# Seven half products for layer 0 too, and sums made in PSUM on a bank already copied out

## The chip, the cores and the metric

One core of a Trainium2 chip runs the whole kernel. The metric is the device time of the program in microseconds (us); lower is better. TensorE multiplies matrices and writes to PSUM[...]; VectorE and ScalarE read PSUM; GpSimd computes a power for the normalizations; SyncE issues the DMAs.

## The reference

There are 32 graphs of 512 nodes with 128 features, and one weighted adjacency matrix `adj` (512 x 512), the same for all graphs. Four layers follow one another, each as `x = x + layer(relu(layernorm(x)))`, all in fp32:

```python
# layer 0: graph convolution
A_hat = adj + eye;  d = A_hat.sum(-1) ** -0.5
out = einsum('nm,bmc->bnc', d[:, None] * A_hat * d[None, :], x) @ W.T + b
# layer 1: gated recurrence, five steps
m = einsum('nm,bmd->bnd', adj, h);  av = concat([m, m])
u3 = h @ u3_w.T + u3_b
z = sigmoid(av @ w3_w.T + w3_b + u3);  r = sigmoid(av @ w4_w.T + w4_b + u3)
hv = tanh(av @ w5_w.T + w5_b + (r * h @ u5_w.T + u5_b));  h = (1 - z) * h + z * hv
# layers 2 and 3: masked attention (softmax over the edges), layer 2 with elu
```

So each graph is multiplied by a 512 x 512 matrix once in layer 0 (normalized adjacency, `anT` in the kernel) and five times in layer 1 (`adj` itself, `adjT`).

## The kernel before, in words

**Plan.** The program is not written in the order in which it runs. Each step is given to `op(engine, cost, due, emit, r, w)`: the engine, an assumed cost in us, a due number, the instruction, what it reads and what it writes. `Plan.run` (lines 81 to 148) then plays the program through once, with these costs and with fixed delays between engines (line 47): whenever an engine is free it takes, of its operations whose inputs are ready and for which a buffer is free, the one with the lowest due number, and among equal ones the one that was given first. That fixes the order of each engine's queue; on the chip each engine runs its queue in that order and waits where an input is late. Buffers are drawn from named lists (lines 170 to 200), among them eight PSUM banks, seven `h`, seven `m`, six `half`, two `S`, three `y`, four `z`, nine `hT`.

**Order of the work.** Lines 712 to 718 give the graphs in 16 pairs `b, b+1`: layer 0 (`gcn`) for each of the two, layer 1 (`ggnn`) for the pair, then the two attention layers (`gat`) for each. Due numbers rise by 10 from pair to pair and by 6 (`LANES`) from one step of layer 1 to the next, and six lanes (one for each graph that is in layer 1) let three pairs be in layer 1 at once. Layer 0 of pair b has due numbers from 5b - 10 on; the first pair's is far earlier. The last four graphs' attention takes a way without DMAs (`near`). 

**Layer 0.** `gcn` (line 470) normalizes x into y (`norm_relu`, one ScalarE instruction for each of four chunks of 128 nodes), adds the bias to x, and calls `product` (line 460): four matmuls of 128 x 128 by 128 x 512 (line 464), one for each chunk of y, are added up in one PSUM bank, and ScalarE copies the bank to m (line 466). Four small matmuls with `w0T` (line 480) and one VectorE add (line 482) finish.

**Layer 1.** `products` (line 503) multiplies the states h of both graphs of a pair at once. Each h is cut into two halves of 256 nodes, and `adjT` into four quarters. Instead of the eight half products that this takes, seven are made, of sums and differences: VectorE makes four sums `S` of halves of the two h (line 515); the right factors are three quarters of `adjT` as they are (`PLAIN`, line 301) and four differences of quarters, made once (`half_adj`, lines 299 to 312). A half product is two matmuls of 128 x 128 by 128 x 256 (line 528) into the low half of a bank. The results are put together as follows; k is the number of the half product:

- bank r1: product 0, copied to `p1` by ScalarE (538); then product 3 is added on top in PSUM, and ScalarE copies the sum to the low half of m1 (544);
- bank r2: product 1; VectorE makes `u2 = p1 + r2` (540). Then product 4 afresh; VectorE makes the high half of m2 as `u4 + r2` (546). Then product 6 on top; the low half of m2 is `u2 + r2` (550);
- bank r3: product 2; `u4 = u2 + r3` (542). Then product 5 on top; the high half of m1 is `u2 + r3` (548).

So a layer-1 product has nine VectorE instructions (four S, five sums) and two ScalarE copies. VectorE's have a due number 5 below that of the matmuls.

`step` (line 553) then makes the gates: matmuls with m and h^T (lines 557 to 572), tanh on ScalarE (560, 566, 574), products on VectorE (562, 576 to 579). The new state goes through VectorE transposes and two rounds of DMA (`shuttle`, line 435) to become the next h.

**Start.** adjT, the degree sums, anT (lines 291 and 294) and the factors of adjT (310, due -6) are made in the first 21 us, while x is still being loaded; the masks of the attention layers follow (323 to 332, due 6 and 7).

Of the kernel before, what the change touches and what calls it, by code (L numbers as in the profile page):

```python
# [14 lines left out]
P = 128  # L15
EPS = 1e-5
STEPS = 5
# [5 lines left out]
LANES = 6  # L23
# [128 lines left out]
def gnn_stack(ctx: ExitStack, tc: tile.TileContext, a: dict, out: bass.AP):  # L152
    nc = tc.nc
    x, adj = a["x"], a["adj"]
    B, N, D = x.shape
    C = N // P
# [6 lines left out]
    def tiles(n, shape, name, pool=sb, dtype=F32):  # L163
        return [pool.tile(shape, dtype, name=f"{name}_{next(serial)}") for _ in range(n)]

    def flat(t):
        return t.rearrange("p c k -> p (c k)")

    TOKENS, SMALL = [P, C, D], [P, C]
# [1 line left out]
        "bank": tiles(8, TOKENS, "bank", psum),  # L171
        "lane": list(range(LANES)),
        "x": tiles(13, TOKENS, "x"),
        "h": tiles(LANES + 1, [P, 2, 2 * D], "h"),
        "sq": tiles(2, [P, Q, W * C], "sq"),
        "far": tiles(4, [Q, W, Q, W * C], "far", dram),
        "hT": tiles(LANES + 3, TOKENS, "hT"),
        "y": tiles(3, TOKENS, "y"),
        "m": tiles(LANES + 1, TOKENS, "m"),
        "S": tiles(2, [P, 4, 2 * D], "S"),  # L180
        "half": tiles(6, [P, 2 * P], "half"),
        "r": tiles(2, TOKENS, "r"),
        "rh": tiles(4, TOKENS, "rh"),
        "z": tiles(4, TOKENS, "z"),
        "hv": tiles(2, TOKENS, "hv"),
        "gT": tiles(2, [P, Q, W * C], "gT"),
        "h_gat": tiles(3, [P, C, D + 3], "h_gat"),
# [13 lines left out]
    op = plan.op  # L201
    MM, MM1, TURN = 0.858, 0.224, 0.111
    V, A = 0.61, 0.585

    def fixed(shape, name, parts=1, dtype=F32):
        v = Val(None, parts)
        v.t = tiles(1, shape, name, dtype=dtype)[0]
        return v
# [81 lines left out]
    for m in range(C):  # L290
# [4 lines left out]
            block(anT.t, m), ident.t, dinv2.t[:, m:m + 1], block(anT.t, m), op0=ALU.mult, op1=ALU.add),  # L295
           r=[ident, dinv2], w=[anT[m]])


    half_adj = fixed([P, 4, 2, 2 * P], "half_adj", 4)
    FACTOR = (None, 1, 0, None, 2, None, 3)  # L300
    PLAIN = {0: (0, 0), 3: (1, 0), 5: (1, 1)}

    def quarter(a, n):
        return adjT.t[:, 2 * a:2 * a + 2, n * 2 * P:(n + 1) * 2 * P]

    def right(k):
        return quarter(*PLAIN[k]) if k in PLAIN else half_adj.t[:, FACTOR[k]]

    for k, u, v in ((2, (0, 1), 0), (1, (1, 1), 2), (4, (1, 1), None), (6, (1, 0), 1)):
        op("DVE", 0.62, -6, lambda k=k, u=u, v=v: nc.vector.tensor_sub(  # L310
            right(k), quarter(*u), quarter(0, 1) if v is None else right(v)),
           r=[adjT, *([half_adj[FACTOR[v]]] if v else [])], w=[half_adj[FACTOR[k]]])


    maskT = {l: fixed([P, Q, N], f"maskT{l}", C, dtype=BF16) for l in (2, 3)}
# [102 lines left out]

    def chunk(h, c):

        if h.kind != "h":
            return h.t[:, c, :]
        return h.t.rearrange("p a (f l) -> p a l f", l=2)[:, c // 2, c % 2, :]

# [10 lines left out]
    def shuttle(src, squares, dst, halves, due, soon):  # L435
# [19 lines left out]
        else:  # L455
            op("SP", 0.4, due, lambda: nc.sync.dma_start(
                dst.t if dst.kind != "h" else dst.t.rearrange("p a (k f) -> p (a k) f", k=2), far.t.rearrange("q i k f -> (q i) k f")),
               r=[far], w=[dst], delay=5)

    def product(h, mT, due):  # L460

        p, m = Val("bank"), Val("m")
        for c in range(C):
            op("PE", MM, due, lambda c=c: nc.tensor.matmul(flat(p.t), chunk(h, c), mT.t[:, c, :], start=(c == 0), stop=(c == C - 1)),  # L464
               r=[h[c] if len(h.writers) > 1 else h, mT[c]], w=[p, m])
        op("ACT", A, due, lambda: nc.scalar.copy(flat(m.t), flat(p.t)), r=[p], w=[m])
        return m


    def gcn(b, due):  # L470
        xb, y = xs[b], Val("y", C)
        norm_relu(b, y, due if b > 1 else 2 * b - 798)
        op("DVE", V, due + 1, lambda: nc.vector.tensor_add(xb.t, xb.t, b0.t[:, None, :].to_broadcast([P, C, D])),
           r=[b0], w=[xb])
        m = product(y, anT, due + 1)
        p = Val("bank")

        def out_mm():
            for c in range(C):
                nc.tensor.matmul(p.t[:, c, :], m.t[:, c, :], w0T.t[:, 0, :], start=True, stop=True)  # L480
        op("PE", C * MM1, due + 2, out_mm, r=[m, w0T], w=[p])
        op("DVE", V, due + 2, lambda: nc.vector.tensor_add(flat(xb.t), flat(xb.t), flat(p.t)), r=[p], w=[xb])


    def ggnn(pair, due):
        hs, hTs, lanes = [], [], []
        for b in pair:
            lane, h, hT = Val("lane"), Val("h", 2), Val("hT")
            op("SP", 0.0, due - 3, lambda: None, r=[xs[b]], w=[lane], delay=0)
            op("SP", 0.0, due - 3, lambda: None, r=[lane], w=[h], delay=0)  # L490
            norm_relu(b, h, due - 3)
            p = to_features(h, due - 2, hT)
            op("ACT", A, due - 2, lambda p=p, hT=hT: nc.scalar.copy(flat(hT.t), flat(p.t)), r=[p], w=[hT])
            hs.append(h)
            hTs.append(hT)
            lanes.append(lane)
        for s in range(STEPS):
            now = due + LANES * s
            ms = products(*hs, now)
            for i, b in enumerate(pair):  # L500
                hs[i], hTs[i] = step(b, s, ms[i], hTs[i], now + i, lanes[i])

    def products(h1, h2, due):

        x1, x2, S = (h1[0], h1[1]), (h2[0], h2[1]), Val("S", 4)
        HV, HM = 0.34, 2 * 0.43

        def part(item):  # L510
            v, a = item
            return v.t[:, a, :]

        def combine(o, u, v, f):
            op("DVE", HV, due - 5, lambda: f(part(o), part(u), part(v)), r=[u, v], w=[o])  # L515
        add, sub = nc.vector.tensor_add, nc.vector.tensor_sub
        combine(S[2], x1[0], x2[0], sub)
        combine(S[0], x2[0], x2[1], add)
        combine(S[1], S[0], x1[0], sub)
        combine(S[3], x1[1], S[1], sub)  # L520
        m1, m2, p1, u2, u4 = Val("m", 2), Val("m", 2), Val("half"), Val("half"), Val("half")
        r1, r2, r3 = Val("bank"), Val("bank"), Val("bank")

        def times(r, item, k, fresh, *also):
            def two():
                u = part(item).rearrange("p (f l) -> p l f", l=2)
                for l in range(2):
                    nc.tensor.matmul(flat(r.t)[:, :2 * P], u[:, l, :], right(k)[:, l, :], start=fresh and l == 0, stop=l == 1,  # L528
                                     skip_group_check=not fresh)
            op("PE", HM, due, two, r=[item, adjT if k in PLAIN else half_adj[FACTOR[k]]], w=[r, *also])  # L530

        def low(v):
            return flat(v.t)[:, :2 * P]

        def high(v):
            return flat(v.t)[:, 2 * P:]
        times(r1, x1[0], 0, True, m1, m2, p1, u2, u4)
        op("ACT", 0.35, due, lambda: nc.scalar.copy(p1.t, low(r1)), r=[r1], w=[p1])  # L538
        times(r2, S[1], 1, True)
        op("DVE", HV, due - 5, lambda: nc.vector.tensor_add(u2.t, p1.t, low(r2)), r=[p1, r2], w=[u2])  # L540
        times(r3, S[0], 2, True)
        op("DVE", HV, due - 5, lambda: nc.vector.tensor_add(u4.t, u2.t, low(r3)), r=[u2, r3], w=[u4])
        times(r1, x1[1], 3, False)
        op("ACT", 0.35, due, lambda: nc.scalar.copy(low(m1), low(r1)), r=[r1], w=[m1[0]])
        times(r2, S[2], 4, True)
        op("DVE", HV, due - 5, lambda: nc.vector.tensor_add(high(m2), u4.t, low(r2)), r=[u4, r2], w=[m2[1]])
        times(r3, S[3], 5, False)
        op("DVE", HV, due - 5, lambda: nc.vector.tensor_add(high(m1), u2.t, low(r3)), r=[u2, r3], w=[m1[1]])
        times(r2, x2[1], 6, False)
        op("DVE", HV, due - 5, lambda: nc.vector.tensor_add(low(m2), u2.t, low(r2)), r=[u2, r2], w=[m2[0]])  # L550
        return m1, m2

    def step(b, s, m, hT, due, lane):
        gate, r, rh, z = Val("bank"), Val("r"), Val("rh"), Val("z")
# [155 lines left out]


    for b in range(0, B, 2):
        gcn(b, STEPS * b - 10)
        gcn(b + 1, STEPS * b - 8)
        ggnn((b, b + 1), STEPS * b)
        for i in range(2):
            gat(b + i, 2, STEPS * (b + i) + LANES * (STEPS - 1) + 3)
            gat(b + i, 3, STEPS * (b + i) + LANES * (STEPS - 1) + 8)
# [32 lines left out]
```

The softmax here doesn't subtract the row's maximum and nothing guards it: scores larger than these inputs give would overflow.

## Time and profile before

| | |
|---|---|
| time, median of 3 runs (range) | 1669.84 us (1669.07 to 1671.38) |
| profiled execution: its own time | 1668.99 us |
| its span, first to last instruction | 1667.2 us |
| mean granted TensorE clock | 0.997 |
| plain products (L464) | 256 matmul records, 593 ns each |
| half products (L528) | 2240 matmul records, 379 to 381 ns each |
| chain that ended last | TensorE 96%, VectorE 3%, ScalarE 1% |

An fp32 matmul stands in the trace as two records; a matmul's duration is longer than its distance to the next one, because they are pipelined. In the lines, "L528 PE MATMUL bank<-half_adj,S" is line 528 of the kernel on TensorE (PE), writing a bank and reading half_adj and S; DVE is VectorE, ACT is ScalarE, PEld the load of the stationary matrix. "x4" means four records. In brackets stands how long the engine was idle before the instruction, and what it waited for. In the table by stretches each engine's busy time follows in its column, then the granted clock.

### The profile page before, as it was taken

What the parts mean: (1) busy time and instruction counts of PE and PEld (TensorE: products, weight loads), DVE (VectorE), ACT (ScalarE), POOL (GpSimd) and SP (SyncE); (2) the same over time, 40 slices, a digit from 0 to 9 for tenths busy, and PEclk for the clock granted to TensorE, in tenths of its full rate; (3) what the DMA queues carried; (4) which work ended last, traced back from release to release, by engine and by line L of the source; (5) the groups of instructions that cost most, each with busy time, mean ns of one, the idle gap of its engine ahead of it and who ended that gap; (6) DMA issues with size and microseconds to landing.
All of it is one profiled execution on the core that took longest, in us unless ns stands there. A gap on an engine that the chain in (4) does not pass through costs nothing.

```text
span 1667.2 us, 23457 instructions
## 1 busy us (share of the span) xinstructions
PE 1645.4 (99%) x7242; PEld 1141.2 (68%) x7242; DVE 1371.1 (82%) x3887; ACT 681.1 (41%) x1467; POOL 143.4 (9%) x136
## 2 busy tenths in 40 slices
PE   8999999999999999999999999999999999999998
PEld 5666656676766776767676676776767767775777
DVE  8866768789887887979889788897988879777988
ACT  5543443435344344443445434344443534334333
POOL 2200001001010010100101010010100001000100
PEclk9999999999999999999999999999999999999999
DMA  5132232353333434343342433424234433434110
GB/s 169 38 73 70 69 92 62 71 135 93 102 85 79 103 86 112 81 100 97 84 115 76 105 92 80 111 75 122 72 94 101 106 87 77 118 77 108 32 33 26
DMA packets 311422, 146.15 MB, mean 88 GB/s; under 512 B 150400, under 2 KB 292864, under 8 KB 311296
## 3 DMA queue, kind: packets, MB, share of 16 engines
q1 hardware_dynamic: 311008, 144.12, 34.3%
q8 instruction: 57, 0.93, 0.2%
q14 instruction: 69, 0.57, 0.1%
q10 hardware_dynamic: 288, 0.52, 0.1%
HBM read 80.48 MB, written 64.08 MB: 87 GB/s over the span
## 4 chain that ended last, share of the span: by engine, by line
PE 96%; DVE 3%; ACT 1%; issue 0%; DMA 0%; DVEq 0%; ACTq 0%
PE bank L528 29%; PE bank L687 11%; PE bank L557 8%; PE bank L571 8%; PE bank L572 8%; PE bank L558 8%; PE bank L564 8%; PE bank L464 6%; PE bank L632 3%; PE bank L480 2%; PE bank L676 1%; PE bank L431 1%; DVE st L389 0%; PE bank L659 0%; DVE e L667 0%; DVE y L415 0%
## 5 line engine op out<-in xcount | busy, mean ns | idle before, releaser
L396 POOL TENSOR_TENSOR rstd<-ve,mhalf 128x4 f32<-128x4 f32 x128 | 141.6, 1108 | 1497.0 <-DVE ve L394 1302.5
L528 PE MATMUL bank<-half_adj,S 128*128 128x256 f32 x960 | 239.6, 381 | 2.2 <-DVE S L515 1.8
L687 PEld LDWEIGHTS bank<-h_gat,e 128*128 128x128 f32 x1792 | 208.6, 191 | 19.4 <-issue 12.8
L560 ACT ACTIVATE r<-bank,gate_bw 128x512 f32<-128x512 f32 x160 | 109.6, 685 | 261.6 <-PE bank L558 226.6
L528 PEld LDWEIGHTS bank<-half_adj,S 128*128 128x128 f32 x960 | 186.1, 197 | 44.2 <-issue 21.4
L687 PE MATMUL bank<-h_gat,e 128*128 128x129 f32 x1792 | 209.3, 275 | 0.7 <-ACT row L654 0.7
L576 DVE TENSOR_TENSOR hv<-hv,hT 128x512 f32<-128x512 f32 x160 | 109.6, 685 | 113.0 <-ACT hv L574 112.7
L667 DVE SCALAR_TENSOR_TENSOR e<-row,h_gat,maskT 128x512 f32<-128x512 f32 x256 | 182.4, 743 | 2.5 <-ACT row L654 2.4
L562 DVE SCALAR_TENSOR_TENSOR rh<-r,hT 128x512 f32<-128x512 f32 x160 | 109.2, 686 | 77.4 <-ACT r L560 76.6
L528 PE MATMUL bank<-adjT,h 128*128 128x256 f32 x640 | 164.9, 380 | 0.8 <-ACT half L538 0.5
L557 PE MATMUL bank<-m,wT 128*128 128x512 f32 x320 | 163.7, 593 | 0.0
L571 PE MATMUL bank<-m,wT 128*128 128x512 f32 x320 | 163.5, 592 | 0.0
L572 PE MATMUL bank<-rh,wT 128*128 128x512 f32 x320 | 163.4, 592 | 0.0
L558 PE MATMUL bank<-hT,wT 128*128 128x512 f32 x320 | 163.4, 592 | 0.0
L564 PE MATMUL bank<-m,wT 128*128 128x512 f32 x320 | 163.2, 593 | 0.0
L406 ACT ACTIVATE y<-x,off,rstd 128x128 f32<-128x128 f32 x352 | 148.2, 483 | 33.0 <-DVE sq L445 17.0
L574 ACT ACTIVATE hv<-bank,gate_bw 128x512 f32<-128x512 f32 x160 | 109.6, 685 | 123.8 <-PE bank L572 123.7
L566 ACT ACTIVATE z<-bank,gate_bw 128x512 f32<-128x512 f32 x160 | 109.5, 685 | 110.2 <-PE bank L564 108.5
L528 PEld LDWEIGHTS bank<-adjT,h 128*128 128x128 f32 x640 | 122.0, 196 | 35.3 <-issue 16.9
L464 PE MATMUL bank<-anT,y 128*128 128x512 f32 x256 | 122.7, 593 | 1.6 <-DVE anT L294 1.6
L389 DVE BATCH_NORM_STATS2 st<-x 128x6 f32<-128x128 f32 x512 | 119.1, 278 | 5.6 <-DMA x<-in_x_dram 5.3
L572 PEld LDWEIGHTS bank<-rh,wT 128*128 128x128 f32 x320 | 60.8, 190 | 76.5 <-issue 64.3
(107 smaller groups left out, 2202.1 us busy)
## 6 DMA issues: line engine op xcount, KB each, us to landing
far<-sq SPq DMA_DIRECT2D x832, 64.0 KB
h<-far SPq DMA_DIRECT2D x248, 128.0 KB
gT<-far SPq DMA_DIRECT2D x56, 256.0 KB
row<-line SPq DMA_DIRECT2D x56, 256.0 KB
x<-in_x_dram SPq DMA_DIRECT2D x32, 256.0 KB
out_dram<-x SPq DMA_DIRECT2D x32, 256.0 KB
h<-far SPq DMA_DIRECT2D x28, 256.0 KB
far_mask<-mask SPq DMA_DIRECT2D x8, 128.0 KB
```

Of the source, the lines that this page charges most:

```text
L389: op("DVE", 0.21, due, lambda c=c: nc.vector.bn_stats(st.t[:, c, :], xb.t[:, c, :]), r=[xb[c]], w=[st[c]])
L396: op("POOL", 1.0, due, lambda: nc.gpsimd.tensor_tensor(rstd.t, ve.t, mhalf.t, ALU.pow), r=[ve, mhalf], w=[rstd])
L406: op("ACT", 0.385, due, lambda c=c: nc.scalar.activation(chunk(y, c), xb.t[:, c, :], AF.Relu, bias=off.t[:, c:c + 1], scale=rstd.t[:, c:c ...
L464: op("PE", MM, due, lambda c=c: nc.tensor.matmul(flat(p.t), chunk(h, c), mT.t[:, c, :], start=(c == 0), stop=(c == C - 1)), r=[h[c] if len ...
L528: nc.tensor.matmul(flat(r.t)[:, :2 * P], u[:, l, :], right(k)[:, l, :], start=fresh and l == 0, stop=l == 1, skip_group_check=not fresh)
L557: nc.tensor.matmul(flat(gate.t), gates.t[:, 0, :], flat(m.t), start=True, stop=False)
L558: nc.tensor.matmul(flat(gate.t), gates.t[:, 1, :], flat(hT.t), start=False, stop=True)
L564: op("PE", MM, due + 0.3, lambda: nc.tensor.matmul(flat(gate.t), gates.t[:, 2, :], flat(m.t), start=False, stop=True, skip_group_check=Tru ...
L571: nc.tensor.matmul(flat(cand.t), gates.t[:, 3, :], flat(m.t), start=True, stop=False)
L572: nc.tensor.matmul(flat(cand.t), u5T.t[:, 0, :], flat(rh.t), start=False, stop=True)
L667: op("DVE", 0.68, due + 3, lambda j=j: nc.vector.scalar_tensor_tensor(e.t[:, j, :], row.t, h.t[:, j, D + 1:D + 2], maskT[l].t[:, j, :], op ...
L687: nc.tensor.matmul(pt()[:, c, :D + 1], e.t[:, j, i * P:(i + 1) * P], h.t[:, j, :D + 1], start=(j == 0), stop=(j == C - 1))
```

## The change

1. The preparation of the four differences becomes a function `right_factors(mT, due)`, which is called for adjT (due -3) and for anT (due -1).
2. `gcn` takes a pair. The first pair goes through `product` as before; every other pair goes through `products` with the factors of anT, with y in a new kind of buffer, `pair`, cut like h.
3. In `products` the seven half products use two banks, r and t, in another order, and three sums are made by PSUM: product 1 is added to product 0 in r, product 2 on top of that, product 5 on top of that, with a ScalarE copy of the bank before each next one. The VectorE adds for `u2` and `u4` and the one for the high half of m1 are gone; the low half of m1 becomes a VectorE add of `p1` and product 3.
4. Assumed costs: half product 0.864 (was 0.86), copy of half a bank 0.26 (was 0.35).
5. Buffers: h 7 to 6, hT 9 to 8, y 3 to 2, z 4 to 3; three `pair` buffers.

```diff
-        times(r1, x1[0], 0, True, m1, m2, p1, u2, u4)
-        op("ACT", 0.35, due, lambda: nc.scalar.copy(p1.t, low(r1)), r=[r1], w=[p1])
-        times(r2, S[1], 1, True)
-        op("DVE", HV, due - 5, lambda: nc.vector.tensor_add(u2.t, p1.t, low(r2)), r=[p1, r2], w=[u2])
-        times(r3, S[0], 2, True)
-        op("DVE", HV, due - 5, lambda: nc.vector.tensor_add(u4.t, u2.t, low(r3)), r=[u2, r3], w=[u4])
-        times(r1, x1[1], 3, False)
-        op("ACT", 0.35, due, lambda: nc.scalar.copy(low(m1), low(r1)), r=[r1], w=[m1[0]])
-        times(r2, S[2], 4, True)
-        op("DVE", HV, due - 5, lambda: nc.vector.tensor_add(high(m2), u4.t, low(r2)), r=[u4, r2], w=[m2[1]])
-        times(r3, S[3], 5, False)
-        op("DVE", HV, due - 5, lambda: nc.vector.tensor_add(high(m1), u2.t, low(r3)), r=[u2, r3], w=[m1[1]])
-        times(r2, x2[1], 6, False)
-        op("DVE", HV, due - 5, lambda: nc.vector.tensor_add(low(m2), u2.t, low(r2)), r=[u2, r2], w=[m2[0]])
+        times(r, x1[0], 0, True, m1, m2, t, p1, u2, u4)
+        copy(p1, r, lambda: p1.t)
+        times(t, x1[1], 3, True)
+        add_up(m1[0], p1, lambda: low(m1))
+        times(r, S[1], 1, False)
+        copy(u2, r, lambda: u2.t)
+        times(t, S[2], 4, True)
+        times(r, S[0], 2, False)
+        copy(u4, r, lambda: u4.t)
+        add_up(m2[1], u4, lambda: high(m2))
+        times(t, x2[1], 6, False)
+        add_up(m2[0], u2, lambda: low(m2))
+        times(r, S[3], 5, False)
+        copy(m1[1], r, lambda: high(m1))
```

with

```python
def copy(o, r, out):
    op("ACT", HA, due, lambda: nc.scalar.copy(out(), low(r)), r=[r], w=[o])
def add_up(o, u, out):
    op("DVE", HV, due - 5, lambda: nc.vector.tensor_add(out(), u.t, low(t)), r=[u, t], w=[o])
```

The other parts, cut:

```diff
-    for k, u, v in ((2, (0, 1), 0), (1, (1, 1), 2), (4, (1, 1), None), (6, (1, 0), 1)):
-        op("DVE", 0.62, -6, lambda k=k, u=u, v=v: nc.vector.tensor_sub(
+    def right_factors(mT, due):
...
+        for k, u, v in ((2, (0, 1), 0), (1, (1, 1), 2), (4, (1, 1), None), (6, (1, 0), 1)):
+            op("DVE", 0.62, due, lambda k=k, u=u, v=v: nc.vector.tensor_sub(
...
+    of_adj, of_an = right_factors(adjT, -3), right_factors(anT, -1)
...
+    def gcn(pair, due):
+        first, ys = pair[0] == 0, []
+        for i, b in enumerate(pair):
+            y = Val("y", C) if first else Val("pair", 2)
+            norm_relu(b, y, 2 * b - 798 if first else due + i)
...
+        ms = [product(y, anT, due + i + 1) for i, y in enumerate(ys)] if first else products(*ys, of_an, due + 1)
...
-        gcn(b, STEPS * b - 10)
-        gcn(b + 1, STEPS * b - 8)
+        gcn((b, b + 1), STEPS * b - 10)
```

In the prediction r0, t3 and so on stand for the half product with that number in bank r or t.

More of the change, by code (lines that the diff above doesn't have):

```diff
@@ L173, in gnn_stack @@
         "x": tiles(13, TOKENS, "x"),
-        "h": tiles(LANES + 1, [P, 2, 2 * D], "h"),
+        "h": tiles(LANES, [P, 2, 2 * D], "h"),
         "sq": tiles(2, [P, Q, W * C], "sq"),
         "far": tiles(4, [Q, W, Q, W * C], "far", dram),
-        "hT": tiles(LANES + 3, TOKENS, "hT"),
-        "y": tiles(3, TOKENS, "y"),
+        "hT": tiles(LANES + 2, TOKENS, "hT"),
+        "y": tiles(2, TOKENS, "y"),
+        "pair": tiles(3, [P, 2, 2 * D], "pair"),
         "m": tiles(LANES + 1, TOKENS, "m"),
@@ L183, in gnn_stack @@
         "rh": tiles(4, TOKENS, "rh"),
-        "z": tiles(4, TOKENS, "z"),
+        "z": tiles(3, TOKENS, "z"),
         "hv": tiles(2, TOKENS, "hv"),
@@ L296, in gnn_stack, with quarter @@
            r=[ident, dinv2], w=[anT[m]])
[L299 to L307, printed above, removed]
-    for k, u, v in ((2, (0, 1), 0), (1, (1, 1), 2), (4, (1, 1), None), (6, (1, 0), 1)):
-        op("DVE", 0.62, -6, lambda k=k, u=u, v=v: nc.vector.tensor_sub(
-            right(k), quarter(*u), quarter(0, 1) if v is None else right(v)),
-           r=[adjT, *([half_adj[FACTOR[v]]] if v else [])], w=[half_adj[FACTOR[k]]])
+    def right_factors(mT, due):
+        made = fixed([P, 4, 2, 2 * P], "made", 4)
+        def quarter(a, n):
+            return mT.t[:, 2 * a:2 * a + 2, n * 2 * P:(n + 1) * 2 * P]
+        f = {0: (lambda: quarter(0, 0), mT), 3: (lambda: quarter(1, 0), mT), 5: (lambda: quarter(1, 1), mT)}
+        f |= {k: (lambda i=i: made.t[:, i], made[i]) for i, k in enumerate((2, 1, 4, 6))}
+        for k, u, v in ((2, (0, 1), 0), (1, (1, 1), 2), (4, (1, 1), None), (6, (1, 0), 1)):
+            op("DVE", 0.62, due, lambda k=k, u=u, v=v: nc.vector.tensor_sub(
+                f[k][0](), quarter(*u), quarter(0, 1) if v is None else f[v][0]()),
+               r=[mT, *([f[v][1]] if v else [])], w=[f[k][1]])
+        return f
+    of_adj, of_an = right_factors(adjT, -3), right_factors(anT, -1)
     maskT = {l: fixed([P, Q, N], f"maskT{l}", C, dtype=BF16) for l in (2, 3)}
@@ L419, in chunk @@
     def chunk(h, c):
-        if h.kind != "h":
+        if h.kind not in ("h", "pair"):
             return h.t[:, c, :]
@@ L458, in shuttle, with products, part, combine @@
                r=[far], w=[dst], delay=5)
+    def products(h1, h2, factors, due):
+        x1, x2, S = (h1[0], h1[1]), (h2[0], h2[1]), Val("S", 4)
+        HV, HM, HA = 0.34, 2 * 0.432, 0.26
+        def part(item):
+            v, a = item
+            return v.t[:, a, :]
+        def combine(o, u, v, f):
+            op("DVE", HV, due - 5, lambda: f(part(o), part(u), part(v)), r=[u, v], w=[o])
+        add, sub = nc.vector.tensor_add, nc.vector.tensor_sub
+        combine(S[2], x1[0], x2[0], sub)
+        combine(S[0], x2[0], x2[1], add)
+        combine(S[1], S[0], x1[0], sub)
+        combine(S[3], x1[1], S[1], sub)
+        m1, m2, p1, u2, u4, r, t = Val("m", 2), Val("m", 2), Val("half"), Val("half"), Val("half"), Val("bank"), Val("bank")
+        def times(r, item, k, fresh, *also):
+            def two():
+                u = part(item).rearrange("p (f l) -> p l f", l=2)
+                for l in range(2):
+                    nc.tensor.matmul(low(r), u[:, l, :], factors[k][0]()[:, l, :], start=fresh and l == 0, stop=l == 1,
+                                     skip_group_check=not fresh)
+            op("PE", HM, due, two, r=[item, factors[k][1]], w=[r, *also])
+        def copy(o, r, out):
+            op("ACT", HA, due, lambda: nc.scalar.copy(out(), low(r)), r=[r], w=[o])
+        def low(v):
+            return flat(v.t)[:, :2 * P]
+        def high(v):
+            return flat(v.t)[:, 2 * P:]
+        def add_up(o, u, out):
[14 more added lines that the diff above has]
+        copy(m1[1], r, lambda: high(m1))
+        return m1, m2
     def product(h, mT, due):
@@ L464, in product, with out_mm @@
             op("PE", MM, due, lambda c=c: nc.tensor.matmul(flat(p.t), chunk(h, c), mT.t[:, c, :], start=(c == 0), stop=(c == C - 1)),
-               r=[h[c] if len(h.writers) > 1 else h, mT[c]], w=[p, m])
+               r=[h[c], mT[c]], w=[p, m])
         op("ACT", A, due, lambda: nc.scalar.copy(flat(m.t), flat(p.t)), r=[p], w=[m])
         return m
[L470 to L482, printed above, removed]
+    def gcn(pair, due):
[3 more added lines that the diff above has]
+            norm_relu(b, y, 2 * b - 798 if first else due + i)
+            op("DVE", V, due + i + 1, lambda b=b: nc.vector.tensor_add(
+                xs[b].t, xs[b].t, b0.t[:, None, :].to_broadcast([P, C, D])), r=[b0], w=[xs[b]])
+            ys.append(y)
+        ms = [product(y, anT, due + i + 1) for i, y in enumerate(ys)] if first else products(*ys, of_an, due + 1)
+        for i, (b, m) in enumerate(zip(pair, ms)):
+            p = Val("bank")
+            def out_mm(m=m, p=p):
+                for c in range(C):
+                    nc.tensor.matmul(p.t[:, c, :], m.t[:, c, :], w0T.t[:, 0, :], start=True, stop=True)
+            op("PE", C * MM1, due + i + 1.5, out_mm, r=[m, w0T], w=[p])
+            op("DVE", V, due + i + 1.5, lambda b=b, p=p: nc.vector.tensor_add(flat(xs[b].t), flat(xs[b].t), flat(p.t)),
+               r=[p], w=[xs[b]])
     def ggnn(pair, due):
@@ L498, in ggnn @@
             now = due + LANES * s
-            ms = products(*hs, now)
+            ms = products(*hs, of_adj, now)
             for i, b in enumerate(pair):
                 hs[i], hTs[i] = step(b, s, ms[i], hTs[i], now + i, lanes[i])
[L503 to L536, printed above, removed]
-        times(r1, x1[0], 0, True, m1, m2, p1, u2, u4)
-        op("ACT", 0.35, due, lambda: nc.scalar.copy(p1.t, low(r1)), r=[r1], w=[p1])
-        times(r2, S[1], 1, True)
-        op("DVE", HV, due - 5, lambda: nc.vector.tensor_add(u2.t, p1.t, low(r2)), r=[p1, r2], w=[u2])
-        times(r3, S[0], 2, True)
-        op("DVE", HV, due - 5, lambda: nc.vector.tensor_add(u4.t, u2.t, low(r3)), r=[u2, r3], w=[u4])
-        times(r1, x1[1], 3, False)
-        op("ACT", 0.35, due, lambda: nc.scalar.copy(low(m1), low(r1)), r=[r1], w=[m1[0]])
-        times(r2, S[2], 4, True)
-        op("DVE", HV, due - 5, lambda: nc.vector.tensor_add(high(m2), u4.t, low(r2)), r=[u4, r2], w=[m2[1]])
-        times(r3, S[3], 5, False)
-        op("DVE", HV, due - 5, lambda: nc.vector.tensor_add(high(m1), u2.t, low(r3)), r=[u2, r3], w=[m1[1]])
-        times(r2, x2[1], 6, False)
-        op("DVE", HV, due - 5, lambda: nc.vector.tensor_add(low(m2), u2.t, low(r2)), r=[u2, r2], w=[m2[0]])
-        return m1, m2
```

## The prediction

> **What bounds the kernel now.** I read the page's busy table first, then the engines by stretches of the span, then TensorE's own instructions in order of time.
>
> ```profile
> PE 1645.4 (99%) x7242; PEld 1141.2 (68%) x7242; DVE 1371.1 (82%) x3887; ACT 681.1 (41%) x1467; POOL 143.4 (9%) x136
> ```
>
> ```profile
> 1000.00:1200.00 200.00, 200.00 (x884) 139.31 (x883) 169.06 (x478) 82.25 (x177) 16.74 (x15) 1.00 0.37 95
> 1500.00:1600.00 100.00, 96.88 (x472) 69.72 (x471) 82.37 (x235) 39.87 (x97) 7.82 (x7) 0.98 0.26 66
> ```
>
> TensorE's column is 200.00 of 200.00 us in the middle, at the full granted clock; VectorE has 15% to spare there, ScalarE 59%. Busy spans overlap because matmuls are pipelined, so "busy" alone proves little. The test is the distance from one start to the next:
>
> ```profile
> 705.32 1.02 PE L557 MATMUL bank<-m,wT 128*128 128x512 f32 x2
> 706.18 1.02 PE L558 MATMUL bank<-hT,wT 128*128 128x512 f32 x2
> ...
> 739.46 1.03 PE L528 MATMUL bank<-half_adj,S 128*128 128x256 f32 x4
> 740.33 1.03 PE L528 MATMUL bank<-adjT,S 128*128 128x256 f32 x4
> ```
>
> A 512-wide product (two records) takes 0.858 us start to start, a half product (two 256-wide products, four records) 0.864. Summed over all records, the excess over these pitches is 0.6 us between 100 and 1500 us, 5.8 us before 40 us, and some 17 us after 1500 us (which includes a half-clock stretch of 3.4 us near 1522 and the drain). So between 40 and 1500 us the time is TensorE's work and nothing else: work taken off it there comes off the span, and any hole costs its length.
>
> **Part 1: layer 0 by pairs.** Fifteen of the sixteen pairs leave the plain product; the first keeps it. Removed: 15 x 8 = 120 products of 512 at 0.858 us = 102.96 us. Added: 15 x 7 = 105 half products at 0.864 = 90.72 us. TensorE gains 12.24 us, 0.8 us a pair. The output products with w0T stay.
>
> On VectorE a pair adds four sums S and three sums into m: 7 x 15 = 105 at 0.41 us (groups L515, L548) = 43 us busy, and four factors from anT at 0.69 (L310) = 2.7 us. On ScalarE two copies of 512 (L466, 0.58) become four of 256 (0.37): 15 x (1.48 - 1.16) = 5 us.
>
> **Part 2: sums made in PSUM.** Each of the 80 layer-1 products loses two VectorE adds (L540, L542, 0.406 us) and gains two ScalarE copies (0.37): VectorE -65 us, ScalarE +59. TensorE's count doesn't change. In all VectorE goes to 1371 - 65 + 46 = 1352 (81%), ScalarE to 681 + 64 = 745 (45%). Neither comes near the bound, so nothing of this is on the path by its sum; at nothing it is covered by TensorE's 99%. What counts is the order it forces.
>
> The seven half products now alternate between two banks, r and t, where three were used. A second use of r waits for ScalarE's copy, of t for VectorE's add; behind the waiting matmul stands all later TensorE work, since its queue runs in order. The price shows where TensorE had nothing else to run:
>
> ```profile
> 1517.80 1.03 PE L528 MATMUL bank<-adjT,h 128*128 128x256 f32 x4
> ...
> 1518.86 0.37 ACT L538 COPY half<-bank 128x256 f32<-128x256 f32 x1 [0.18 <-PE bank L528]
> ...
> 1519.28 1.14 PE L528 MATMUL bank<-adjT,h 128*128 128x256 f32 x4 [0.46 <-ACT half L538]
> ```
>
> From one use of a bank to the next over a ScalarE copy: 1.48 us (over a VectorE add, 1525.50 to 1527.05, 1.55). With one half product in the other bank between, 1.73 us pass, so r0-t3-r1-t4-r2 runs without a hole. Then it doesn't: t6 waits for m2's add, which waits for the copy of r2's sum, and r5 waits for that copy too. Both follow r2 directly, so an isolated product stalls 1.48 - 0.86 = 0.62 us there. Before, r2 and r3 alternated at that point and had none. Bounds: 0 if other ready matmuls fill it, 0.62 x 95 products = 59 us if none ever does.
>
> [...] The width costs 0.864 against 0.858 by the rows, which is in the sum. For the rotation I go by the rows on how long a product lies ready:
>
> ```profile
> 724.12 0.42 DVE L515 TENSOR_TENSOR S<-h,S 128x256 f32<-128x256 f32 x1
> ...
> 734.30 1.03 PE L528 MATMUL bank<-half_adj,S 128*128 128x256 f32 x4
> ```
>
> The last S was ready at 724.54; TensorE came to it 9.8 us later. Over the repeating stretch from 300 to 1300 us this wait is 4.2 to 21.6 us for every product. So other ready work stands beside each product, and the scheduler, which picks another ready operation when one waits, has something for a 0.62 us hole. I take 0 for the middle. Only six of the first eight products and the last five have waits below 4 us. There 0.62 each is exposed, but each also loses two adds of 0.34 us pitch from VectorE's queue, on which those stretches wait (S at 1522: 1.77 us; half at 1527: 0.41). 0.62 against 0.68: I take 0, with both ends, -3 and +6 us, for the range.
>
> **Part 3: the head.** The full products of graphs 2 to 5 are TensorE's filler while the first pair goes through its chain:
>
> ```profile
> 26.98 1.10 PE L464 MATMUL bank<-anT,y 128*128 128x512 f32 x2
> 27.92 1.03 PE L528 MATMUL bank<-adjT,h 128*128 128x256 f32 x4
> 28.79 3.60 PE L464 MATMUL bank<-anT,y 128*128 128x512 f32 x8
> 32.22 0.63 PE L431 MATMUL bank<-ident,h 128*128 128x128 f32 x4
> ```
>
> They start as soon as one chunk of one graph is normalized. The paired product needs both graphs (y of graph 3 is complete at 32.9 us), the four S, and the factors of anT, and VectorE is 96% to 99% busy from 20 to 62 us. The factors (due -1) go ahead of the statistics of graphs 2 and 3 (due 0 and 1): 4 x 0.60 pitch = 2.4 us later for those. So the block at 28.79 has no replacement: four products, 3.4 us. Below, 0, if other work moves up; above, the fillers at 51.6 to 58.5 us (5.2 us) go too, as VectorE has about 5 us more to do by then. I take 3.4, the row that is directly gone. SP's queue gains no DMA: loads are issued as before.
>
> **Part 4: buffers.** h 7 to 6, hT 9 to 8, y 3 to 2, z 4 to 3, pair 3 new. An h lives inside a lane, of which there are six, so the seventh was idle. y loses most of its users to pair: layer 0 was a third of them. z lives from its tanh to the second VectorE step, 4.4 us (711.14 to 715.54), while a graph-step takes 101.1/10 = 10 us of the repeating pattern: three suffice. In the end stretch eight y's pass through two buffers instead of three; the transposes that free them take 0.6 us, so 0 to 2 us, taken as 0.
>
> **Sum.** Profiled execution 1668.99 us: -12.24 + 3.4 = 1660.2. The median of the runs shown lies 0.85 above it, so **1661.0 us**, 0.5% less.
>
> **Rivals.**
> *All of the gain.* The planner finds other filler at the head, and the end is no worse: 1669.84 - 12.24 = 1657.6; with a better end, 1655. For: of VectorE's 41 us from 20 to 62 us, 4.5 are masks and a part of the 21 us of statistics is for later graphs, which can wait. Against: its 98% there. Chance 0.2.
> *The head and the end take most of it.* Head 3.4 + 5.2 = 8.6, of which a third is filled by other work, leaves 5.7; thin cover 11 x 0.62 = 6.8, of which VectorE's relief gives half back, leaves 3.4: 1657.6 + 5.7 + 3.4 = 1666.7. For: the end already has 17 us of holes. Chance 0.25.
> *The bank chain is exposed in the middle (slower).* Place: after r2 in each product, where ScalarE's copy must come first; price 0.62 us, more where a 0.69 us tanh lies ahead of the copy on ScalarE. From (12.24 - 3.4)/0.62 = 14 uncovered products of 95 on it eats the gain; at 20 the kernel is slower by 0.2%, and with all, 1657.6 + 59 = 1717. For: layer 0's plain products were themselves filler (1026.4, 1029.8 and 1034.1 us are single pieces between dependent steps). Against: the 4 to 22 us waits above. Chance 0.05.
>
> **How the numbers follow.** 1661.0 with 0.5 (own range 1659 to 1664), and the three rivals with 0.2, 0.25 and 0.05. The range 1656 to 1667 leaves out the better part of the first rival's end, the worst of the second and the third: 2 in 10. A measurement of this kernel can tell 0.2%, 3.3 us, from no change: faster means below 1666.5. Slower takes 0.04 of the third; same, 0.07, is the second's upper end and a piece of the third; the rest, 0.89, is faster.
>
> **What would show it.** Right: TensorE's records fall by 240 at the plain product and rise by 420 half ones; the middle keeps 200.00 of 200.00; the repeating pattern shrinks from 101.1 to about 100.3 us; new holes stand before 60 us. Wrong: waits of half products on the ScalarE copy in the repeating stretch (the third rival), or a head without new holes (the first), or an end that grows by over 3 us.

## The result and the profile after

The changed kernel takes 1663.66 us (median of 6 runs, 1662.76 to 1664.75), the kernel before 1669.86 us in the same comparison: a ratio of 0.9962, 95% interval 0.9949 to 0.9975. That is 6.2 us faster where 8.9 us were forecast. The profiled execution took 1663.59 us, its span 1661.8 us.

The busy table of the page after:

```profile
PE 1634.7 (98%) x7422; PEld 1176.3 (71%) x7422; DVE 1362.7 (82%) x3836; ACT 734.8 (44%) x1657; POOL 143.2 (9%) x136
```

TensorE has 180 records more, as the prediction counted (-240 + 420). VectorE is at 1363 us (forecast 1352), ScalarE at 735 us (745): both as far from the bound as before. The table by stretches of the span, cut at the stages (busy time of PE, PEld, DVE, ACT, POOL, then granted clock, DMA share, GB/s), first of the kernel before, then of the changed one:

```profile
20.00:60.00 40.00, 38.94 (x146) 23.69 (x145) 39.16 (x186) 24.93 (x58) 13.53 (x13) 1.00 0.38 103
60.00:1490.00 1430.00, 1430.00 (x6102) 981.61 (x6101) 1174.23 (x3238) 583.09 (x1231) 111.68 (x100) 1.00 0.36 90
```

```profile
20.00:60.00 40.00, 36.51 (x156) 26.63 (x155) 39.23 (x165) 24.43 (x59) 10.20 (x10) 1.00 0.35 97
60.00:1490.00 1430.00, 1427.89 (x6325) 1020.26 (x6324) 1172.26 (x3234) 633.92 (x1411) 114.36 (x104) 1.00 0.36 91
```

The middle, which had not a hole in 1430 us, now has some. Busy time understates them, since a matmul's modelled end reaches into the hole. So I add up, as in the prediction, what each start-to-start distance of matmul records exceeds the usual one of its kind; a stretch at a lower granted clock counts in it too. All kernels of this study by this measure, each in its one profiled execution, in us (the second column is the median of all runs):

| kernel | median us | 0-20 | 20-60 | 60-1490 | 1490-1600 | from 1600 |
|---|---|---|---|---|---|---|
| before | 1669.86 | 3.2 | 2.3 | 0.6 | 6.2 | 11.0 |
| changed | 1663.66 | 3.0 | 5.6 | 5.1 | 5.9 | 9.8 |
| psum_only | 1678.74 | 3.1 | 2.3 | 1.1 | 4.1 | 20.6 |
| pairs_only | 1660.90 | 3.1 | 6.0 | 1.8 | 6.9 | 9.7 |
| inplace | 1661.56 | 3.2 | 6.5 | 1.7 | 6.8 | 12.0 |
| third_bank | 1659.63 | 3.1 | 5.8 | 1.6 | 4.2 | 11.0 |
| head_factors_late | 1666.63, one run | 3.2 | 7.0 | 6.6 | 6.0 | 10.1 |
| head_two_pairs_plain | 1669.60, one run | 3.2 | 6.1 | 8.5 | 5.9 | 10.2 |
| head_both | 1664.64, one run | 2.9 | 3.0 | 8.7 | 6.0 | 9.8 |
| inplace_head_S3 | 1655.55 | 3.3 | 2.4 | 1.1 | 3.2 | 10.2 |
| cost_only | 1674.24 | 3.6 | 6.4 | 5.1 | 6.5 | 19.3 |

The values from 20 to 60 us of pairs_only, inplace, third_bank, the first two head kernels and cost_only contain a stretch at a lower granted clock: their tables by stretches read 0.96 from 20 to 60 us (0.91 from 20 to 40 us in the two head kernels), where the changed kernel reads 1.00. At half the clock, which the traces of before and of the changed kernel show in such stretches, that is some 3.4 us, an estimate; 1.5 to 1.75 us of their excess lie in it. After 1490 us every kernel has such stretches: 4.5 us at half the clock in the changed kernel and 8.9 before, and by an estimate from the mean granted clock from 1490 to 1655 us (0.96 and 0.94, against 0.99 and 0.98 in those two) some 13 us in cost_only and 20 in psum_only.

From before to changed: -12.2 of work, +3.3 from 20 to 60 us, +4.5 in the middle, -1.5 after 1490 us, which leaves -5.9; the spans differ by 5.4. The rest, 0.5, was not traced.

The head, TensorE in order of time, first one more line of the kernel before, then the changed one:

```profile
25.20 1.48 PE L528 MATMUL bank<-adjT,h 128*128 128x256 f32 x4 [0.29 <-ACT h L406]
```

```profile
26.23 1.48 PE L485 MATMUL bank<-adjT,h 128*128 128x256 f32 x4 [1.45 <-ACT h L407]
27.54 0.63 PE L432 MATMUL bank<-ident,h 128*128 128x128 f32 x4
28.01 1.04 PE L485 MATMUL bank<-adjT,h 128*128 128x256 f32 x4
29.27 0.39 PE L432 MATMUL bank<-ident,h 128*128 128x128 f32 x1 [0.22 <-ACT h L407]
30.03 0.77 PE L432 MATMUL bank<-ident,h 128*128 128x128 f32 x3 [0.38 <-ACT h L407]
```

Where the block of plain products stood at 28.79 us there is nothing, and TensorE takes each piece of the second graph's h as it comes. The first hole was not foreseen: h of the first graph is itself 1 us later.

A hole in the middle, all engines in order of time:

```profile
146.76 2.86 PE L485 MATMUL bank<-made,S 128*128 128x256 f32 x12
...
149.66 0.37 ACT L490 COPY half<-bank 128x256 f32<-128x256 f32 x1 [1.46 <-PE bank L485]
...
150.07 0.42 DVE L498 TENSOR_TENSOR m<-half,bank 128x256 f32<-128x256 f32 x1 [2.14 <-ACT half L490]
150.09 1.14 PE L485 MATMUL bank<-adjT,S 128*128 128x256 f32 x4 [0.46 <-ACT half L490]
```

This is the stall that the prediction derived: the third product in bank r ends, ScalarE copies (149.66 to 150.03), product 5 (adjT,S) follows at 150.09. From the start of the last half product of the first row (148.60 by its records) to that of product 5, 1.49 us pass, against 0.864: 0.62 us of hole. All 7422 records of TensorE start in the order in which the plan gave TensorE its operations (so do the 7242 of the kernel before): nothing from behind product 5 went ahead of it. There are eight holes of over 0.15 us in the middle. Six wait like this one for the copy of r (0.17 to 0.65 us; the shorter ones have a part covered by transposes), one holds product 6 until the VectorE add, and one holds layer 0's output product until the last copy into m. The prediction had the size of a whole one right and took none of them as exposed.

### The profile page after: what moved, and what is told of

It is laid out like the page before. It is cut to its first block, busy times and chain, and to the rows that moved or that the text cites. A ratio compares the mean times of both kernels' runs of the same rounds, so it can differ in the third digit from the quotient of the medians.

```text
span 1661.8 us, 23750 instructions
## 1 busy us (share of the span) xinstructions
PE 1634.7 (98%) x7422; PEld 1176.3 (71%) x7422; DVE 1362.7 (82%) x3836; ACT 734.8 (44%) x1657; POOL 143.2 (9%) x136
## 4 chain that ended last, share of the span: by engine, by line
PE 92%; DVE 5%; ACT 1%; issue 1%; DMA 0%; POOL 0%; SPq 0%; DVEq 0%; POOLq 0%; ACTq 0%
PE bank L485 33%; PE bank L699 12%; PE bank L570 8%; PE bank L569 8%; PE bank L576 8%; PE bank L583 8%; PE bank L584 8%; PE bank L644 3%; PE bank L541 2%; PE bank L688 1%; PE bank L432 1%; DVE st L390 1%; PE bank L520 0%; ACT y L407 0%; POOL rstd L397 0%
## 5 line engine op out<-in xcount | busy, mean ns | idle before, releaser
L485 PE MATMUL bank<-made,S 128*128 128x256 f32 x1140 | 276.3, 380 | 3.9 <-DVE S L473 1.8
L485 PEld LDWEIGHTS bank<-made,S 128*128 128x128 f32 x1140 | 218.1, 196 | 45.5 <-issue 19.0
L490 ACT COPY half<-bank 128x256 f32<-128x256 f32 x285 | 105.3, 370 | 256.9 <-PE bank L485 254.9
L485 PE MATMUL bank<-adjT,h 128*128 128x256 f32 x640 | 157.8, 380 | 1.5 <-ACT h L407 1.5
L498 DVE TENSOR_TENSOR m<-half,bank 128x256 f32<-128x256 f32 x285 | 117.6, 413 | 43.2 <-ACT half L490 22.8
L570 PEld LDWEIGHTS bank<-hT,wT 128*128 128x128 f32 x320 | 60.8, 190 | 76.5 <-issue 76.5
```

The source lines that it names most:

```text
L485: nc.tensor.matmul(low(r), u[:, l, :], factors[k][0]()[:, l, :], start=fresh and l == 0, stop=l == 1, skip_group_check=not fresh)
L498: op("DVE", HV, due - 5, lambda: nc.vector.tensor_add(out(), u.t, low(t)), r=[u, t], w=[o])
L570: nc.tensor.matmul(flat(gate.t), gates.t[:, 1, :], flat(hT.t), start=False, stop=True)
```

## Experiments

The question was why these stalls are exposed although, by the trace of before, every product lies ready for 4 us or more. The code suggests a reason that the wait of inputs doesn't show: a product takes three `half` buffers when it begins, and there are six, so at most two products are open. While both wait, a third may not begin, though its first half product needs nothing but h. Theory A: a forced stall, where nothing may start. Theory A': the half buffers are what forbids it. The rivals: the copies cost by themselves (B), VectorE is late (B2), or only layer 0's plain products are missed as filler, work that could run in the holes (C).

**psum_only.** Layer 0 plain in all pairs (shown in part; `gcn` is that of before again, with three `y` buffers and no `pair`):

```diff
-        gcn((b, b + 1), STEPS * b - 10)
+        gcn(b, STEPS * b - 10)
+        gcn(b + 1, STEPS * b - 8)
```

> Part 2 alone: sums in PSUM in layer 1, layer 0 plain for all pairs (y buffers three, as before). Theory A (a hole after the third product in bank r opens only where TensorE finds no other operation that it may start; plain layer-0 products are such operations): no holes between 60 and 1500 us, TensorE's work as before, head as before, so 1670 us, with 3 us either way from the end. Theory B (the alternation of two banks costs by itself, in ScalarE's copies): the middle holds the 5.1 us of holes that the changed kernel has, so 1675 us.

1678.74 us, ratio to before 1.0058 (1.0041 to 1.0075). Its middle:

```profile
60.00:1490.00 1430.00, 1430.00 (x6120) 982.35 (x6119) 1127.57 (x3084) 628.70 (x1380) 111.09 (x99) 1.00 0.36 90
```

By starts it has 1.1 us of holes: 80 products with the two-bank order, and none of their stalls is exposed. Theory B falls. But the time missed the forecast by 9 us: the end has 24.7 us of holes instead of 17.2. TensorE in order of time there:

```profile
1616.63 1.94 PE L431 MATMUL bank<-ident,hT 128*128 128x128 f32 x8 [2.10 <-DVE hT L584]
1623.10 2.09 PE L681 MATMUL bank<-h_gat,e 128*128 128x129 f32 x8 [4.53 <-DVE e L672]
...
1648.84 1.44 PE L681 MATMUL bank<-h_gat,e 128*128 128x129 f32 x5 [5.43 <-DVE e L672]
```

TensorE waits 4.5 and 5.4 us for VectorE's attention scores (e) of the last graphs, and part of the rest is the lower clock named above. What sends the drain, the last stretch in which no new graphs come, this way is the question of cost_only.

**pairs_only.** Layer 0 by pairs; in all products the body, the three banks and the VectorE sums of before:

```diff
-        times(r, x1[0], 0, True, m1, m2, t, p1, u2, u4)
-        copy(p1, r, lambda: p1.t)
...
+        times(r1, x1[0], 0, True, m1, m2, p1, u2, u4)
+        op("ACT", 0.35, due, lambda: nc.scalar.copy(p1.t, low(r1)), r=[r1], w=[p1])
+        times(r2, S[1], 1, True)
...
```

> Part 1 alone: layer 0 by pairs, all products with three banks and the sums on VectorE as before; VectorE gets some 55 us more of sums than before. Theory A: the 12.24 us of TensorE's work are gone, the head's loss of 3 us stays, no holes in the middle: 1663.7 - 5 = 1658.7 us, 3 us either way from the end. Theory B2 (VectorE, at 86%, becomes late instead): holes in the middle of 5 us or more that wait for VectorE, 1664 us or above. If the holes of the changed kernel come from layer 0 by pairs itself (rival C: filler gone), they are here too: 1663.7 us.

1660.90 us, ratio 0.9950 (0.9935 to 0.9965). The stretch table and the page's busy line:

```profile
60.00:1490.00 1430.00, 1430.00 (x6330) 1020.43 (x6330) 1226.17 (x3426) 575.79 (x1248) 115.96 (x106) 1.00 0.36 91
```

```profile
PE 1636.1 (99%) x7422; PEld 1177.1 (71%) x7422; DVE 1417.2 (85%) x4026; ACT 666.9 (40%) x1467; POOL 143.5 (9%) x136
```

No gap in busy time in the middle (1.8 us by starts), with VectorE at 85%. B2 falls, and C alone too: the plain products are gone here as well. It takes both parts: part 1 removes the filler that needs no half buffer, part 2 makes the stall that needs filler. On top of part 1, part 2 relieves VectorE, which isn't needed, and adds holes to the middle, 5.1 against 1.8 us. By time alone the two kernels can't be told apart: their intervals overlap.

**inplace.** ScalarE copies into m1 and m2, VectorE adds there; no half buffers:

```diff
-        times(r, x1[0], 0, True, m1, m2, t, p1, u2, u4)
-        copy(p1, r, lambda: p1.t)
+        times(r, x1[0], 0, True, m1, m2, t)
+        copy(m1[0], r, lambda: low(m1))
...
-        add_up(m1[0], p1, lambda: low(m1))
+        add_up(m1[0], lambda: low(m1))
```

and so for u2 (low half of m2) and u4 (high half of m2); `add_up` becomes `tensor_add(out(), out(), low(t))`.

> The changed kernel, but ScalarE copies r's partial sums straight into their place in m1 and m2, and VectorE adds t there in place; the pool of six half buffers is gone. Same instructions, same banks, same waits between them. Theory A': the holes open because every further product has to wait for three of the six half buffers, so that no product can start while two are open: without the pool the middle's 5.1 us of holes fall to about 1 us, 1659.6 us, 3 us either way from the end. Theory B (the copies' latency or ScalarE's queue): nothing changes in the middle, 1663.7 us.

1661.56 us, ratio 0.9957 (0.9943 to 0.9972). The middle's holes fall from 5.1 to 1.7 us with the same instructions, banks and waits:

```profile
60.00:1490.00 1430.00, 1429.52 (x6323) 1021.17 (x6322) 1173.83 (x3246) 635.67 (x1414) 112.10 (x104) 1.00 0.36 91
```

So the half buffers were what kept other products from filling the stalls: A' holds. By time alone it isn't shown, since the intervals overlap. In the profiled execution head and end gave back 1 and 3 us, but it was the slowest of four (1664.02 us, mean granted clock 0.997; the others 0.999 to 1.000).

The plan shows the same. `Plan.run` needs no chip, and it was played through again from the code of each kernel. This is its own model, not a measurement. For the changed kernel it leaves eight gaps of over 0.1 us in TensorE's queue between 60 and 1490 us, 4.4 us in all. In each of them the first half product of one or two other pairs is ready and lacks three half buffers, and nothing else is ready. The plans of psum_only and pairs_only have no gap there. With nine half buffers and nothing else altered 0.8 us are left, as in the plan of inplace. On the chip a larger pool was not tried.

**third_bank.** Products 3 and 6 in a bank of their own, order r0 t4 r1 s3 r2 s6 r5, one add more:

```diff
-        times(t, x1[1], 3, True)
-        add_up(m1[0], p1, lambda: low(m1))
+        times(t, S[2], 4, True)
         times(r, S[1], 1, False)
         copy(u2, r, lambda: u2.t)
-        times(t, S[2], 4, True)
+        times(s, x1[1], 3, True)
+        add_up(m1[0], p1, lambda: low(m1), s)
         times(r, S[0], 2, False)
         copy(u4, r, lambda: u4.t)
-        add_up(m2[1], u4, lambda: high(m2))
-        times(t, x2[1], 6, False)
-        add_up(m2[0], u2, lambda: low(m2))
+        add_up(u2, u2, lambda: u2.t, t)
+        add_up(m2[1], u4, lambda: high(m2), t)
+        times(s, x2[1], 6, True)
+        add_up(m2[0], u2, lambda: low(m2), s)
         times(r, S[3], 5, False)
```

> The changed kernel, but product 3 and then product 6 have a bank s of their own, and the order is r0 t4 r1 s3 r2 s6 r5, so that each two uses of a bank have another product between them that waits for nothing younger; VectorE makes one add more per product (u2 + t), 95 x 0.41 = 39 us busy in all. Theory A: the forced 0.62 us stall after r2 is gone, whether or not other work is ready: middle's holes from 5.1 to below 1 us, 1659 us, 3 us either way from the end. Theory B (a pool of half buffers alone, whatever the order, or VectorE's load): holes stay or grow, 1663.7 us or above.

1659.63 us, ratio 0.9942 (0.9927 to 0.9957). The middle:

```profile
60.00:1490.00 1430.00, 1429.79 (x6313) 1020.65 (x6312) 1197.34 (x3327) 642.63 (x1426) 112.93 (x104) 1.00 0.36 91
```

By starts its holes fall to 1.6 us with the half buffers still six. The forced stall is the other necessary part: take away either and the holes go. VectorE's 25 us more in this stretch (1197.34 against 1172.26) cost nothing that shows.

**The head**, three kernels with one run each, for the holes from 20 to 60 us. The first has the factors of anT later:

```diff
-    of_adj, of_an = right_factors(adjT, -3), right_factors(anT, -1)
+    of_adj, of_an = right_factors(adjT, -3), right_factors(anT, 5)
```

> The changed kernel with the factors of anT due 5 instead of -1. If the head's loss (5.6 us of holes from 20 to 60 us against 2.3 before) comes from the factors going ahead of other work on VectorE, the hole of 1.6 us near 24.5 us (TensorE waits for h of the first graph) shrinks to the 0.45 us of before and the stretch has 4.4 us; if it comes only from the missing plain products, it stays at 5.6 us or grows, since the second pair's product then waits for its factors.

The second (head_two_pairs_plain) leaves the second pair plain too (shown in part; `y` buffers three, `pair` two):

```diff
-        first, ys = pair[0] == 0, []
+        first, ys = pair[0] < 4, []
...
-            norm_relu(b, y, 2 * b - 798 if first else due + i)
+            norm_relu(b, y, 2 * b - 798 if pair[0] == 0 else due + i)
```

> The changed kernel with the second pair plain as well (TensorE gets 0.82 us more; y buffers three, pair two). If the missing plain products alone make the head's loss, the stretch from 20 to 60 us falls from 5.6 to about 3 us; if the factors' place on VectorE makes it, the 1.6 us hole near 24.5 us stays, and the rest falls by 2 us at most.

The third (head_both) has both edits:

> Both edits of the head together: second pair plain and the factors of anT due 5. Both accounts of the head: 2.3 to 2.9 us of holes from 20 to 60 us, as before the change. The middle has the two-open-products limit still, so 4 to 8 us of holes there. If VectorE's load by itself (all its sums and statistics) makes the head's loss, the stretch stays near 5 us.

TensorE in order of time, in this order of the kernels:

```profile
24.95 1.48 PE L485 MATMUL bank<-adjT,h 128*128 128x256 f32 x4 [0.27 <-ACT h L407]
...
31.47 1.88 PE L485 MATMUL bank<-made,S 128*128 128x256 f32 x4 [1.98 <-DVE S L473]
```

```profile
26.25 2.07 PE L485 MATMUL bank<-adjT,h 128*128 128x256 f32 x4 [1.46 <-ACT h L407]
```

```profile
24.78 1.48 PE L485 MATMUL bank<-adjT,h 128*128 128x256 f32 x4 [0.27 <-ACT h L407]
...
27.44 4.46 PE L520 MATMUL bank<-anT,y 128*128 128x512 f32 x10
31.73 0.63 PE L432 MATMUL bank<-ident,h 128*128 128x128 f32 x4
```

Late factors alone bring the first hole back from 1.45 to 0.27 us, but then TensorE runs dry before 31.47 us: 7.0 us in the stretch. The plain second pair alone leaves the first hole: 6.1 us. 1.6 us of each of these two sums lie in the stretch at the lower clock (0.91 from 20 to 40 us, 1.00 in the changed kernel). Together the edits give 3.0 us, against 5.6 for the change and 2.3 before. Neither cause alone accounts for the head's loss; it is the factors' place on VectorE and the missing filler. Their times of one run bear no finer reading, and their middles, which keep the half buffers, have 6.6 to 8.7 us of holes.

**inplace_head_S3.** Sums in place, a third S buffer in the freed room, both edits of the head (`pair` buffers two, y three).

```diff
-        "S": tiles(2, [P, 4, 2 * D], "S"),
-        "half": tiles(6, [P, 2 * P], "half"),
+        "S": tiles(3, [P, 4, 2 * D], "S"),
```

> The version to which the theory points: sums in place (no half buffers), a third S buffer from the room that this frees, second pair plain, factors of anT due 5. TensorE's work as in the changed kernel but 0.82 us more; holes from 60 to 1490 us 5.1 to 1.5 us, head 5.6 to 2.6 us; the end is the unknown, from 12 to 20 us of holes. 1663.7 + 0.8 - 3.6 - 3.0 = 1657.9 us, 4 us either way. Rival: holes only move to other places, 1663 us.

1655.55 us, ratio to before 0.9919 (0.9903 to 0.9936): faster than both kernels. Its stretches:

```profile
20.00:60.00 40.00, 38.99 (x154) 26.09 (x152) 38.68 (x171) 24.62 (x58) 11.80 (x11) 1.00 0.38 104
60.00:1490.00 1430.00, 1429.95 (x6309) 1019.90 (x6308) 1162.94 (x3238) 641.12 (x1420) 123.91 (x105) 1.00 0.36 91
```

Head 2.4, middle 1.1 us of holes, as before the change, with 11.4 us less work; the end, 13.4 us, is 3.8 better than before, and that part was not aimed at.

**cost_only.** One number that the plan assumes, and no instruction:

```diff
-        HV, HM, HA = 0.34, 2 * 0.432, 0.26
+        HV, HM, HA = 0.34, 2 * 0.432, 0.35
```

> The changed kernel with one assumed cost altered, ScalarE's copy of half a bank 0.35 us as before instead of 0.26; no instruction, buffer or dependency differs, only the order that the plan makes. Theory D (the holes of the end, 17 us before, 16 after, 25 with part 2 alone, are decided by the order in which the last graphs happen to come, not by what the change does): the end moves by several us in either direction while the middle keeps about 5 us of holes: 1660 to 1672 us, more than 2 us from the changed kernel. Rival: the end is set by the last graphs' work itself, and the time stays within 1 us of 1663.7.

1674.24 us (9 runs), ratio to before 1.0024 (1.0014 to 1.0035): slower than before, 10.6 us above the changed kernel. The middle is the same (5.1 us), the end has 25.8 us of holes against 15.7. TensorE's waits after 1490 us (us in total, how many, the longest):

```profile
PE bank L688 <- DVE e L679: 7.1, 3, 5.3
PE bank L432 <- DVE y L416: 3.0, 1, 3.0
PE bank L432 <- DVE hT L591: 2.2, 1, 2.2
```

In the changed kernel the longest wait in this stretch is 1.8 us. So the order in which the last graphs fall out of the plan decides some 10 us, more than the change itself brings, and in this kernel the assumed cost of 0.26 is worth nearly as much as the 12.2 us of saved matmuls. Theory D holds. The plan tells it without a chip: by its own clock it ends at 1656.9 us for the changed kernel, 1666.0 for cost_only, 1669.3 for psum_only and 1661.2 for the kernel before. Its differences from the changed kernel, 9.1, 12.4 and 4.3 us, stand beside measured ones of 10.6, 15.1 and 6.2.

## Why the prediction came out as it did

- **TensorE's work, -12.24 us**: right. Records as counted; the repeating pattern shrank from 101.1 us to 100.4 (909.2 to 1210.5 us is three of them), forecast 100.3.
- **The head, +3.4 us**: right in size (5.6 - 2.3 = 3.3), half right in cause. The block at 28.79 us had no replacement; besides, the factors delayed h of the first graph by 1 us, not only the statistics of graphs 2 and 3. That first hole grew from 0.29 to 1.45 us, a third of the 3.3, so the match of the sums is in part luck.
- **The forced stall, 0.62 us**: right to the hundredth where the whole of it is exposed (0.62 us at 149 us, 0.65 at 1311).
- **Its cover, "I take 0 for the middle"**: this step failed. The argument was "other ready work stands beside each product, and the scheduler ... has something for a 0.62 us hole", from waits of 4.2 to 21.6 us. Those waits show ready inputs. An operation also needs free buffers, and with two products open the others lack the half buffers. The runs showed eight holes in place of none, 4.5 us more than before; the plan, played through, shows them too. third_bank, in which products 3 and 6 have a bank of their own, closes the holes. The upper bound of 59 us was far from what came, 4.5.
- **The few products with thin cover, "I take 0"**, and **y's buffers at 0**: from 1490 us on the change has 1.5 us less holes. The end is, by cost_only, a matter of order, so this neither confirms nor refutes the balance of 0.62 against 0.68.
- **The rivals**: all of the gain didn't come; of "the bank chain is exposed in the middle" the mechanism came, at 8 places instead of the 20 from which it would have been slower. Its argument for itself, that layer 0's plain products were filler, is what psum_only shows.
- **The uncertainty of the end**, -3 to +6 us, was too small: against 17.2 us of holes before, 13.4 to 25.8 were seen for nearly the same work. That the total still fell near the forecast owes something to the end, which here gave 1.5 us back.

## What to carry to other kernels

A long wait between ready inputs and execution is not yet cover for a stall: ask what else an operation must take to start, and count how many can be open at once. When a change shortens steady work by less than 1%, look at the fill and the drain of the pipeline separately, and compare kernels there stage by stage, because an order that a plan happens to make can move more than the change. Where the program makes its plan itself, play it through for both kernels first: its gaps, what was ready in them and for which buffer it waited can be read before any run. Work without dependencies that looks merely wasteful may be what fills the holes of the rest.

## What was not expected of the hardware

In the traces of the kernel before and of the changed one the granted clock is full except in stretches of 3.41 us at one half (the last of each is cut by the end of the span): from 1521.79, 1644.67 and 1665.15 us before, from 1640.23 and 1660.71 us in the changed kernel. The first begins in a hole of 1.77 us, shorter than itself, and the half product behind that hole spread over 2.05 us instead of 1.03:

```profile
1522.19 2.05 PE L528 MATMUL bank<-half_adj,S 128*128 128x256 f32 x4 [1.77 <-DVE S L515]
```

In head_factors_late TensorE had nothing from about 29.5 to 31.47 us. The half product at 31.47 us spread over 1.88 us, and the row of its table by stretches reads 0.91:

```profile
20.00:40.00 20.00, 17.01 (x72) 13.07 (x71) 18.55 (x84) 10.29 (x26) 4.00 (x4) 0.91 0.26 74
```

The hole of 1.98 us thus cost some 3.6 us, an estimate: the hole and the 1.6 us of excess in the starts behind it.

The length of one hole does not decide it. The hole of 1.46 us before 26.25 us in head_two_pairs_plain has a stretch at the lower clock with it (2.07 us for the half product behind it, 0.91 from 20 to 40 us). The same hole in the changed kernel, 1.45 us before 26.23 us, has none (1.48 us, 1.00), nor have its holes of 1.29, 1.62 and 1.80 us before 1502.19, 1519.87 and 1612.77 us. In the two traces named first the edges of the halved stretches lie whole multiples of 3.413 us apart (1521.79 and 1644.67 us before: 36 of them; 1640.23 and 1660.71 us in the changed kernel: 6). The idle time within one such step does not decide it either: by the modelled ends it was 1.55 us in one step with a halved stretch behind it (the changed kernel, 1636.82 to 1640.23 us) and 1.80 us in another without (1609.51 to 1612.92 us). What decides stays open.
